# Layer 3's experts: parts of 112 and 64, and blocks finished in pairs

## The chip, the cores and the metric

The kernel runs on one core of a Trainium2 chip. The metric is the device time of one execution in microseconds (us). Before the change it is 716.23 us (median of 3 runs, 713.53 to 717.75). The experts that the change touches work in fp32.

## What is computed

A stack of four layers, each an attention or graph step and a feed-forward step, on x of 4 x 256 tokens with 256 features. The change touches only the last feed-forward step, a mixture of experts with one shared branch. On the 1024 normalized rows:

```python
H = 256; I_MOE = 176; I_SH = 704; E = 8; TOP_K = 2
probs = softmax(x @ W_router.T)
rw, sel = top_k(probs, TOP_K)
combine = zeros((T, E)).at[arange(T)[:, None], sel].add(rw)
sh = silu_and_mul(x @ Ws_gate_up, I_SH) @ Ws_down
shared_out = sh * sigmoid(x @ W_sgate.T)
gu = einsum('th,ehi->eti', x, We_gate_up)        # 2 * 176 columns
h = silu_and_mul(gu, I_MOE)                      # 176 columns
eo = einsum('eti,eih->eth', h, We_down)          # contracts over 176
out = shared_out + einsum('eth,te->th', eo, combine)
```

Each token goes to two of eight experts. An expert's hidden width is 176. Layer 2 has a step of the same kind with a hidden width of 128.

## The kernel before

**Stages.** The layers run one after the other, with some overlap at the borders. Layer 3's feed-forward step comes last: routing, a dispatch that sorts the 2048 token-expert pairs into blocks of 128 rows with one expert each, the experts over these blocks, and the shared branch, pieces of which run before and after the experts.

**Units.** `experts` (L378) does one block per unit; there are NB = 23 of them, numbered 0 to 22. A unit has four pieces:

- `load` (L382): SyncE reads the expert's number and starts the load of its weights (`d_w`, six buffers); GpSimd gathers the 128 rows by an indirect DMA (`d_x`, six buffers, L397); TensorE transposes them in two halves (L402), and one copy empties the bank into `d_xT`.
- `up`: two matmuls of 128 rows and 352 columns (the helper at L217), silu of the first 176 columns on ScalarE (L412), times the other 176 on VectorE (L413): `d_h`, 128 tokens by 176.
- `turn_round`: `d_h` must be contracted over its 176 columns, so they have to be put on partitions. There are only 128 of these, so the 176 are cut into `parts` = 2 halves of `hs` = 88. Two transposes (L420) write the halves side by side into one bank of PSUM, 88 partitions by 256 columns, and one copy empties both into `d_hT` (three buffers).
- `down`: two matmuls of 88 rows and 256 columns (L430) add up the halves in one bank, a copy takes the result to `d_y`, and GpSimd writes the rows out by an indirect DMA (L439).

The pieces are skewed: in step s TensorE gets load(s), up(s-1), turn_round(s-2), down(s-3). TensorE's order is written out by hand for this part of the kernel (`in_order`), and it waits in that order. The other engines' orders come from the tile framework's scheduler, and the waits on semaphores from its tracking of tiles.

**Copies out of PSUM.** `evac` (L104 to L111) alternates between VectorE (L109) and ScalarE (L111) with each call. In layer 3 a unit calls it three times. All eight banks of PSUM are handed out in turn by `bank()`.

**Weights.** `_blocks` on the host lays an expert's weights out as one block of 128 partitions by 1216 columns: 704 for up, and two times 256 for the two halves of down. Layer 2 uses the same functions with one part of 128 and its weights resident in SBUF.

Of the kernel before, what the change touches and what calls it, by code (L numbers as in the profile page):

```python
# [27 lines left out]
P = 128  # L28
# [5 lines left out]
E = 8  # L34
# [4 lines left out]
TOPK2 = int(S * 0.3)  # L39
SH2, RT2 = 1024, 128  # L40
SH3, RT3 = 704, 176
RH3 = RT3 // 2
ROUND = 12582912.0
NEG = -1.0e30
LOWEST = -3.0e38
# [20 lines left out]
def flamingo(ctx: ExitStack, tc: tile.TileContext, a: dict, out: bass.AP):  # L66
# [191 lines left out]
    class Dispatch:  # L258
# [118 lines left out]
        def experts(self, src, ff, parts, between, resident=None):  # L377


            hs, width = ff // parts, KC * 2 * ff + parts * D  # L380
            state = {}

            def load(n):
                first = nc.values_load(
                    self.of[0:1, n : n + 1], min_val=0, max_val=(E - 1) * P,
                    engines=[mybir.EngineType.SP if resident is None else mybir.EngineType.PE],
                    skip_runtime_bounds_check_because="the number of experts is clamped to E - 1 above",
                )
                if resident is None:
                    w = self.pool.tile([P, width], F32, tag="d_w", name="d_w", bufs=6)  # L390
                    nc.sync.dma_start(w, src[bass.ds(first, P), :])
                    cols = lambda c0, n: w[:, c0 : c0 + n]
                else:
                    first = first * (width // P)
                    cols = lambda c0, n: resident[:, bass.ds(first + c0, n)]
                xb = self.pool.tile([P, D], F32, tag="d_x", name="d_x", bufs=6)
                nc.gpsimd.indirect_dma_start(  # L397
                    out=xb, out_offset=None, in_=rows_in, in_offset=self.indices(self.token[:, n : n + 1])
                )
                pt = bank()[:, :D]  # L400
                for kc in range(KC):
                    nc.tensor.transpose(pt[:, kc * P : (kc + 1) * P], xb[:, kc * P : (kc + 1) * P], ident)  # L402
                xbT = self.pool.tile([P, KC, P], F32, tag="d_xT", name="d_xT", bufs=3)
                evac(xbT.rearrange("p k t -> p (k t)"), pt)
                state[n] = cols, xbT

            def up(n):
                cols, xbT = state[n]
                pg = bank()[:, : 2 * ff]
                project(pg, lambda kc: xbT[:, kc, :], lambda kc: cols(kc * 2 * ff, 2 * ff))  # L410
                hb = self.pool.tile([P, ff], F32, tag="d_h", name="d_h", bufs=3)
                nc.scalar.activation(hb, pg[:, :ff], AF.Silu)  # L412
                nc.vector.tensor_mul(hb, hb, pg[:, ff:])  # L413
                state[n] = cols, hb

            def turn_round(n):
                cols, hb = state[n]
                pt = bank()[:, : parts * P]
                for c in range(parts):
                    nc.tensor.transpose(pt[:hs, c * P : (c + 1) * P], hb[:, c * hs : (c + 1) * hs], ident)  # L420
                hbT = self.pool.tile([P, parts * P], F32, tag="d_hT", name="d_hT", bufs=3)
                evac(hbT[:hs], pt[:hs])
                state[n] = cols, hbT

            def down(n):
                cols, hbT = state.pop(n)
                po = bank()[:, :D]
                for c in range(parts):
                    c0 = KC * 2 * ff + c * D
                    nc.tensor.matmul(  # L430
                        po, hbT[:hs, c * P : (c + 1) * P], cols(c0, D)[:hs], start=c == 0, stop=c == parts - 1
                    )
                y = self.pool.tile([P, D], F32, tag="d_y", name="d_y", bufs=5)
                if not self.scatter:
                    nc.scalar.copy(y, po)
                    nc.scalar.dma_start(rows_out[n * P : (n + 1) * P, :], y)
                    return
                evac(y, po)
                sent = nc.gpsimd.indirect_dma_start(  # L439
                    out=rows_out, out_offset=self.indices(self.to[:, n : n + 1]), in_=y, in_offset=None  # L440
                )
                if n:
                    tc.declare_no_dep(sent.ins, group=self.name, reason="all pairs have rows of their own")
                tc.add_to_no_dep_group(self.name, sent.ins)

            for step in range(NB + 3):
                for lag, piece in enumerate((load, up, turn_round, down)):
                    if 0 <= step - lag < NB:
                        piece(step - lag)
                between(step)  # L450
# [1389 lines left out]
def _blocks(up, down):  # L1840


    n = up.shape[2]
    out = np.zeros((E, P, KC * n + down.shape[1] * D), np.float32)
    out[:, :, : KC * n] = up.reshape(E, KC, P, n).transpose(0, 2, 1, 3).reshape(E, P, KC * n)
    out[:, : down.shape[2], KC * n :] = down.transpose(0, 2, 1, 3).reshape(E, down.shape[2], -1)
    return out.reshape(E * P, -1)


def _layout(i):  # L1850
    ctx = i["ctx_512"].reshape(B * S, C)
    cw = np.zeros((C, CW_END), np.float32)
    cw[:, CW_KV0 : CW_KV0 + C] = i["L0_xattn_W_k"].T
    bk = np.zeros((P, C + 1), np.float32)
    bk[:, :C] = i["L0_xattn_b_k"]
    bk[D1::32, C] = 1.0
    wkv, wq = i["L1_xattn_Wkv_expand"], i["L1_xattn_Wq"]
    wq1 = np.zeros((D, 4 * P), np.float32)
    for h in range(H1):
        rows = slice(h * D1, (h + 1) * D1)  # L1860
        k0 = 32 * h
        cw[:, CW_K1 + k0 : CW_K1 + k0 + D1] = wkv[rows].T
        wq1[:, k0 : k0 + D1] = wq[rows].T
    cw[:, CW_V1:] = wkv[D:].T
    cw[:, CW_Q2 : CW_Q2 + C] = i["L2_xattn_Wq"].T
    cw[:, CW_K2 : CW_K2 + C] = i["L2_xattn_Wk"].T

    router = np.zeros((D, 3, 32), np.float32)
    router[:, 0, :E] = i["L0_ffn_gate_w"]
    router[:, 1, :E] = i["L2_ffn_router_w"].T  # L1870
    router[:, 2, :E] = i["L3_ffn_W_router"].T
    router[:, 2, E : E + 1] = i["L3_ffn_W_sgate"].T
    had = np.ones((1, 1), np.float32)
    while had.shape[0] < P:
        had = np.block([[had, had], [had, -had]])

    kT = np.zeros((2, 4, 32, B * S), np.float32)
    kT[:, :, :D3] = ctx.T.reshape(2, 4, D3, B * S)
    kT[:, :, D3] = 1.0
    va = np.zeros((B * S, KV3, 32), np.float32)  # L1880
    va[:, :, :D3] = ctx.reshape(B * S, KV3, D3)
    va[:, :, D3] = 1.0

    w12, w3 = i["L2_ffn_w12"], i["L2_ffn_w3"]
    gu, dn = i["L3_ffn_We_gate_up"], i["L3_ffn_We_down"]
    sgu = i["L3_ffn_Ws_gate_up"]
    ew = i["L0_ffn_expert_w"].reshape(E // 2, 2, KC, P, D).transpose(0, 3, 2, 1, 4)
    a = {
        "x": i["x"],
        "ctxT": ctx.reshape(2, 2, S, C).transpose(1, 3, 0, 2).reshape(P, 2, S),  # L1890
        "cw": np.concatenate([cw, cw]),
        "bk": bk,
        "g_xattn": i["g_xattn"],
        "g_ffn": i["g_ffn"],
        "ln_gamma": i["L0_xattn_ln_gamma"],
        "ln_beta": i["L0_xattn_ln_beta"],
        "router": router.reshape(KC, P, -1).transpose(1, 0, 2),
        "gate_b": i["L0_ffn_gate_b"],
        "expert_bias": i["L2_ffn_expert_bias"],
        "gamma_raw": i["L2_xattn_gamma_raw"].reshape(1),  # L1900
        "hadamard": had,
        "expert_w": ew.reshape(E // 2, P, KC * 2 * D),
        "expert_b": i["L0_ffn_expert_b"].reshape(E * D),
        "l1_wq": _kc(wq1),
        "l1_wo": _kc(i["L1_xattn_Wout"].T),
        "l1_w0": i["L1_ffn_w_gate"].T.reshape(KC, P, FF1),
        "l1_w1": i["L1_ffn_w_up"].T.reshape(KC, P, FF1),
        "l1_w2": i["L1_ffn_w_down"].T.reshape(2, 4, P, D).transpose(0, 2, 1, 3).reshape(2, P, FF1),
        "l3_kT": kT.reshape(2, P, B * S).transpose(1, 0, 2),
        "l3_v": va.reshape(NT, P, KV3, 32).transpose(1, 0, 2, 3),  # L1910
        "ffn2_s": _chunks((i["L2_ffn_sw1"].T, i["L2_ffn_sw2"].T), i["L2_ffn_sw3"].T, CHUNKS2S),
        "ffn2_r": _blocks(w12.transpose(0, 2, 1), w3.transpose(0, 2, 1).reshape(E, 1, RT2, D)),
        "ffn3_s": _chunks((sgu[:, :SH3], sgu[:, SH3:]), i["L3_ffn_Ws_down"], CHUNKS3S),
        "ffn3_r": _blocks(gu, dn.reshape(E, 2, RH3, D)),
    }
    return {n: np.ascontiguousarray(v) for n, v in a.items()}

# [16 lines left out]
```

## Time and profile before

| what | us |
|---|---|
| median of 3 runs | 716.23 |
| lowest, highest | 713.53, 717.75 |
| the profiled execution | 717.04 |
| its span in the profile | 715.3 |
| TensorE matmuls busy | 661.3 (92%) |
| VectorE busy | 463.8 (65%) |
| ScalarE busy | 320.2 (45%) |
| GpSimd busy | 191.8 (27%) |

The span runs from the first to the last instruction on the core; the rest of the execution's time lies around it. A matmul in fp32 is shown as two records, a transpose as one. Each record's length includes its way through the array, so records of one engine overlap; how fast they follow each other is read from their starts, or from the chain of waits, which shows each only up to where the next one takes over. PEld is the load of the stationary operand. A form such as 88*128 88x256 is a matmul with 88 rows, 128 stationary columns and 256 moving ones. L217 is a helper's line and stands for several uses, which are told apart by the tiles' names.

Layer 3's experts run from about 625 us to 683 us of the span. The groups of that stretch that the change touches:

| line, engine, tile | form | count | mean ns of one |
|---|---|---|---|
| L420 PE b<-ident,d_h | 128*88 128x128 | 46 | 273 |
| L430 PE b<-d_w,d_hT | 88*128 88x256 | 92 | 379 |
| L109 VectorE d_hT<-b | 88x256 | 12 | 421 |
| L111 ScalarE d_hT<-b | 88x256 | 11 | 367 |

### The profile page before, as it was taken

What the parts mean: (1) busy time and instruction counts of PE and PEld (TensorE: products, weight loads), DVE (VectorE), ACT (ScalarE), POOL (GpSimd) and SP (SyncE); (2) the same over time, 40 slices, a digit from 0 to 9 for tenths busy, and PEclk for the clock granted to TensorE, in tenths of its full rate; (3) what the DMA queues carried; (4) which work ended last, traced back from release to release, by engine and by line L of the source; (5) the groups of instructions that cost most, each with busy time, mean ns of one, the idle gap of its engine ahead of it and who ended that gap; (6) DMA issues with size and microseconds to landing.
All of it is one profiled execution on the core that took longest, in us unless ns stands there. A gap on an engine that the chain in (4) does not pass through costs nothing.

```text
span 715.3 us, 12096 instructions
## 1 busy us (share of the span) xinstructions
PE 661.3 (92%) x4239; PEld 395.2 (55%) x4239; DVE 463.8 (65%) x1305; ACT 320.2 (45%) x702; POOL 191.8 (27%) x270
## 2 busy tenths in 40 slices
PE   6799999889987699799999989999989998999998
PEld 3434436466655476645887457554534443677745
DVE  5798999866986688857342566787857536533334
ACT  3667764644572455631243210565655653133310
POOL 2334474122232101160651430000010001367420
PEclk9869999999997899999999998999988999999999
DMA  7400113100001300020363122200000000779833
GB/s 240 184 0 1 44 40 94 46 3 25 2 2 46 154 1 0 31 89 1 110 147 91 51 77 73 82 16 19 2 31 3 2 1 31 253 244 325 290 94 113
DMA packets 26564, 54.70 MB, mean 76 GB/s; under 512 B 5004, under 2 KB 15976, under 8 KB 26248
## 3 DMA queue, kind: packets, MB, share of 16 engines
q1 hardware_dynamic: 18680, 39.38, 16.5%
q0 software_dynamic: 4080, 11.15, 5.6%
q10 hardware_dynamic: 3744, 3.41, 1.4%
q8 instruction: 34, 0.56, 0.3%
q14 instruction: 26, 0.21, 0.1%
HBM read 43.48 MB, written 9.19 MB: 74 GB/s over the span
## 4 chain that ended last, share of the span: by engine, by line
PE 65%; DVE 15%; ACT 9%; POOL 4%; issue 3%; DMA 2%; SPq 2%; ACTq 0%; POOLq 0%; DVEq 0%
PE b L217 19%; PE b L551 7%; PE b L1638 5%; PE b L1622 5%; PE b L1583 5%; PE b L956 4%; PE b L430 4%; PE b L1102 3%; ACT xn L198 2%; ACT pT L1274 2%; DVE max L1590 2%; DVE ln_st L182 1%; DVE g_work L627 1%; SPq L1579 1%; PE b L402 1%
## 5 line engine op out<-in xcount | busy, mean ns | idle before, releaser
L217 PE MATMUL b<-xnT,w 128*128 128x512 f32 (+2 forms) x288 | 113.5, 547 | 2.1 <-ACT xnT L111 1.2
L1590 DVE TENSOR_REDUCE max<-b 128x2 f32<-128x512 f32 x128 | 80.8, 682 | 25.1 <-PE b L1622 22.7
L1629 ACT ACTIVATE pT<-b 128x512 f32<-128x512 f32 x128 | 69.1, 601 | 45.8 <-PE b L1622 45.1
L217 PEld LDWEIGHTS b<-xnT,w 128*128 128x128 f32 (+1 forms) x288 | 52.7, 187 | 53.5 <-issue 48.3
L1583 PE MATMUL b<-kT,qT 32*128 32x256 f32 x512 | 72.2, 418 | 2.0 <-DMA qT<-xnT 1.5
L1622 PE MATMUL b<-qT,kT 32*128 32x512 f32 x256 | 73.4, 671 | 0.4 <-DMA qT<-rows 0.4
L956 PE MATMUL b<-w,xnT 128*128 128x512 f32 x128 | 63.9, 656 | 0.0
L397 POOL DMA_INDIRECT d_x<-rows_in,d_token x46 | 44.2, 960 | 64.8 <-DVE d_tok L373 21.3
L1583 PEld LDWEIGHTS b<-kT,qT 32*128 32x128 f32 x512 | 43.2, 193 | 23.8 <-issue 14.6
L551 PE MATMUL b<-w,hT 128*128 128x256 f32 x224 | 55.4, 401 | 0.0
L551 PEld LDWEIGHTS b<-w,hT 128*128 128x128 f32 x224 | 42.6, 197 | 13.1 <-issue 6.7
L1638 PE MATMUL b<-pT,va 128*32 128x256 f32 x512 | 42.4, 400 | 2.5 <-ACT pT L1629 2.5
L956 PEld LDWEIGHTS b<-w,xnT 128*128 128x128 f32 x128 | 26.1, 210 | 33.0 <-issue 33.0
L198 ACT ACTIVATE xn<-x,ln_shift,ln_rstd 128x256 f32<-128x256 f32 x56 | 29.3, 592 | 33.6 <-POOL ln_shift L190 33.6
L1666 POOL TENSOR_TENSOR x<-x,att 128x256 f32<-128x256 f32 x8 | 5.6, 725 | 133.2 <-DVE att L1662 90.4
L1102 PE MATMUL b<-had,zT 128*128 128x256 f32 x128 | 32.1, 406 | 9.0 <-ACT zT L1093 7.4
L972 POOL TENSOR_TENSOR re<-re 128x512 f32<-128x512 f32 (+1 forms) x32 | 33.0, 1035 | 26.3 <-ACT re L964 25.1
L1226 DVE TENSOR_REDUCE m<-b 128x3 f32<-128x384 f32 x64 | 31.1, 549 | 13.2 <-PE b L1219 13.0
L189 POOL TENSOR_TENSOR ln_rstd<-ln_ve,neghalf 128x4 f32<-128x4 f32 (+1 forms) x15 | 14.8, 985 | 91.6 <-DVE ln_shift L187 91.3
L510 DVE TENSOR_TENSOR hT<-b,sil 128x512 f32<-128x512 f32 (+1 forms) x22 | 15.2, 689 | 34.0 <-PE b L217 27.4
L509 ACT ACTIVATE sil<-b 128x512 f32<-128x512 f32 (+1 forms) x22 | 13.1, 594 | 53.7 <-PE b L217 52.1
L1278 POOL TENSOR_SCALAR_AFFINE_SELECT pT<-pT 128x512 f32<-128x512 f32 x32 | 19.6, 637 | 59.9 <-ACT pT L1274 59.9
(320 smaller groups left out, 1264.4 us busy)
## 6 DMA issues: line engine op xcount, KB each, us to landing
d_w<-in_ffn_r_dram SPq DMA_DIRECT2D x23, 608.0 KB
w<-in_ffn_s_dram SPq DMA_DIRECT2D x13, 384.0 KB
w<-in_l_w_dram SPq DMA_DIRECT2D x6, 512.0 KB
d_wall<-in_ffn_r_dram SPq DMA_DIRECT2D x1, 3072.0 KB
rows_out<-d_y ACTq DMA_DIRECT2D x23, 128.0 KB
w<-in_expert_w_dram SPq DMA_DIRECT2D x4, 512.0 KB
rows_in<-xn SPq DMA_DIRECT2D x16, 128.0 KB
d_yt<-rows_out SPq DMA_DIRECT2D x8, 256.0 KB
```

Of the source, the lines that this page charges most:

```text
L198: nc.scalar.activation(xn, x[t0 + i], AF.Identity, bias=shift[:, i : i + 1], scale=rstd[:, i : i + 1])
L217: nc.tensor.matmul(dst, lhs(kc), rhs(kc), start=kc == 0, stop=kc == KC - 1)
L397: nc.gpsimd.indirect_dma_start(out=xb, out_offset=None, in_=rows_in, in_offset=self.indices(self.token[:, n : n + 1]))
L551: nc.tensor.matmul(po, hT[:hs, j, i * P : (i + 1) * P], w[:hs, 4 * hs : 4 * hs + D], start=j == 0, stop=j == len(ws) - 1,)
L956: nc.tensor.matmul(pe, xt[:, kc, i * P : (i + 1) * P], ws0[j][:, kc * 2 * D : (kc + 1) * 2 * D], start=False, stop=kc == KC - 1,)
L972: nc.gpsimd.tensor_add(re[:, :n, :], re[:, :n, :], re[:, n : 2 * n, :])
L1102: nc.tensor.matmul(pf[:, c // 2, (c % 2) * 2 * P : (c % 2 + 1) * 2 * P], self.zT[:, c0 : c0 + P], had2[:, n].rearrange("p s q -> p (s q)") ...
L1583: nc.tensor.matmul(pn[:, half * S : (half + 1) * S], self.qT[group(k), ah, g0 + half, qt * P : (qt + 1) * P], kT[group(k), ah, self.b * S ...
L1590: nc.vector.tensor_reduce(self.max[:, ah, qt, k, g0 : g0 + 2], pn.rearrange("p (g s) -> p g s", g=2), AX.X, ALU.max, negate=True,)
L1622: nc.tensor.matmul(pn, kT[group(k), ah, c : c + P], self.qT[group(k), ah, g0 : g0 + 2, :], start=True, stop=True)
L1629: nc.scalar.activation(self.pT[u][:, k, :], pn, AF.Exp, scale=D3**-0.5)
L1638: nc.tensor.matmul(self.acc[group(k), cols], va[:, 2 * self.b + kt, 4 * ah + k, :], self.pT[u][:, k, cols], start=kt == 0 and g == 0, stop ...
```

## The change

The 176 columns are cut into 112 and 64 instead of 88 and 88 (`first_part`). The second part of an even unit goes to partitions 0 to 63, that of an odd unit to partitions 64 to 127 (`rows`). For an odd unit the second part is written as a plain matmul with the identity as the moving operand, all other parts as transposes. Each part has a copy of its own, right after it, and `d_hT` gets four buffers.

`down` does nothing for an even unit, and in the next step does two units together: the two first parts, and then the two second parts, each in its own half of the rows of TensorE's array and in its own bank. The last unit, number 22, has no partner and is done alone. The host puts the second part's weights into both halves of the partitions. The size of a weight block, the number of loads, gathers and writes, and the order on GpSimd and SyncE stay the same. For layer 2 (one part) nothing changes.

```diff
@@ -39,7 +39,6 @@
 TOPK2 = int(S * 0.3)
 SH2, RT2 = 1024, 128
 SH3, RT3 = 704, 176
-RH3 = RT3 // 2
 ROUND = 12582912.0
 NEG = -1.0e30
 LOWEST = -3.0e38
@@ -377,7 +376,15 @@
         def experts(self, src, ff, parts, between, resident=None):
 
 
-            hs, width = ff // parts, KC * 2 * ff + parts * D
+            width = KC * 2 * ff + parts * D
+            first_part = ff - P // 2 * (parts - 1)
+
+            def rows(n, c):
+
+
+                r = P // 2 * (n % 2) if c else 0
+                return slice(r, r + (ff - first_part if c else first_part))
+
             state = {}
 
             def load(n):
@@ -416,20 +423,35 @@
             def turn_round(n):
                 cols, hb = state[n]
                 pt = bank()[:, : parts * P]
+                hbT = self.pool.tile([P, parts * P], F32, tag="d_hT", name="d_hT", bufs=4)
                 for c in range(parts):
-                    nc.tensor.transpose(pt[:hs, c * P : (c + 1) * P], hb[:, c * hs : (c + 1) * hs], ident)
-                hbT = self.pool.tile([P, parts * P], F32, tag="d_hT", name="d_hT", bufs=3)
-                evac(hbT[:hs], pt[:hs])
+                    part = rows(n, c), slice(c * P, (c + 1) * P)
+                    src = hb[:, c * first_part : ff if c else first_part]
+                    if part[0].start:
+                        nc.tensor.matmul(pt[part], src, ident, start=True, stop=True)
+                    else:
+                        nc.tensor.transpose(pt[part], src, ident)
+                    evac(hbT[part], pt[part])
                 state[n] = cols, hbT
 
             def down(n):
-                cols, hbT = state.pop(n)
-                po = bank()[:, :D]
+                if parts == 2 and n % 2 == 0 and n + 1 < NB:
+                    return
+                some = (n - 1, n) if parts == 2 and n % 2 else (n,)
+                pos = [bank()[:, :D] for _ in some]
                 for c in range(parts):
-                    c0 = KC * 2 * ff + c * D
-                    nc.tensor.matmul(
-                        po, hbT[:hs, c * P : (c + 1) * P], cols(c0, D)[:hs], start=c == 0, stop=c == parts - 1
-                    )
+                    for m, po in zip(some, pos):
+                        cols, hbT = state[m]
+                        r = rows(m, c)
+                        nc.tensor.matmul(
+                            po, hbT[r, c * P : (c + 1) * P], cols(KC * 2 * ff + c * D, D)[r],
+                            start=c == 0, stop=c == parts - 1,
+                        )
+                for m, po in zip(some, pos):
+                    del state[m]
+                    store(m, po)
+
+            def store(n, po):
                 y = self.pool.tile([P, D], F32, tag="d_y", name="d_y", bufs=5)
                 if not self.scatter:
                     nc.scalar.copy(y, po)
@@ -1840,10 +1862,15 @@
 def _blocks(up, down):
 
 
-    n = up.shape[2]
-    out = np.zeros((E, P, KC * n + down.shape[1] * D), np.float32)
+    n, ff = up.shape[2], down.shape[1]
+    parts = -(-ff // P)
+    first = ff - P // 2 * (parts - 1)
+    out = np.zeros((E, P, KC * n + parts * D), np.float32)
     out[:, :, : KC * n] = up.reshape(E, KC, P, n).transpose(0, 2, 1, 3).reshape(E, P, KC * n)
-    out[:, : down.shape[2], KC * n :] = down.transpose(0, 2, 1, 3).reshape(E, down.shape[2], -1)
+    out[:, :first, KC * n : KC * n + D] = down[:, :first]
+    if parts == 2:
+        for r in (0, P // 2):
+            out[:, r : r + P // 2, KC * n + D :] = down[:, first:]
     return out.reshape(E * P, -1)
 
 
@@ -1909,9 +1936,9 @@
         "l3_kT": kT.reshape(2, P, B * S).transpose(1, 0, 2),
         "l3_v": va.reshape(NT, P, KV3, 32).transpose(1, 0, 2, 3),
         "ffn2_s": _chunks((i["L2_ffn_sw1"].T, i["L2_ffn_sw2"].T), i["L2_ffn_sw3"].T, CHUNKS2S),
-        "ffn2_r": _blocks(w12.transpose(0, 2, 1), w3.transpose(0, 2, 1).reshape(E, 1, RT2, D)),
+        "ffn2_r": _blocks(w12.transpose(0, 2, 1), w3.transpose(0, 2, 1)),
         "ffn3_s": _chunks((sgu[:, :SH3], sgu[:, SH3:]), i["L3_ffn_Ws_down"], CHUNKS3S),
-        "ffn3_r": _blocks(gu, dn.reshape(E, 2, RH3, D)),
+        "ffn3_r": _blocks(gu, dn),
     }
     return {n: np.ascontiguousarray(v) for n, v in a.items()}
```

## The prediction

> **What bounds the kernel now.** First the chain of waits over the last 115 us, because the change sits in layer 3's experts and nowhere else. One unit of that stage in the steady part, with two pieces of the shared FFN around the stage for comparison:
>
> ```profile
> 608.14 5.96 PE b L551 x24
> ...
> 643.65 1.19 PE b L217 x4
> 644.84 0.22 PE b L420 x2
> 645.06 0.86 PE b L430 x4
> 645.92 0.22 PE b L402 x2
> ...
> 682.93 17.31 PE b L217 x40
> 700.24 11.94 PE b L551 x48
> ```
>
> Start, length, what ran, records. From 625.42 to 682.93 the chain is almost only TensorE: 23 units, each load (L402) 0.22, up (L217) 1.19, turn (L420) 0.22, down (L430) 0.865, in all 2.49 us. A 256-column fp32 matmul is two records of 0.216, a transpose one of 0.109. So a microsecond added to or taken from TensorE's order here moves the end. Next the table of stretches, for what lies just beneath:
>
> ```profile
> core 0: us, PE busy (x) PEld busy (x) DVE busy (x) ACT busy (x) POOL busy (x), PEclk, DMA share, GB/s
> 641.00:661.00 20.00, 20.00 (x99) 14.83 (x98) 7.48 (x21) 6.81 (x20) 15.13 (x16) 1.00 1.00 335
> ```
>
> TensorE is busy throughout, at clock 1.00; VectorE and ScalarE a third of the time; but the DMA engines are full too. A unit moves 608 KB of weights and two times 128 KB of rows: at 335 GB/s that is 2.64 us. There is a second bound close under the first.
>
> **What the change takes away.** Down becomes one pass for two units: two 112-row matmuls (four records, 0.864), then two 64-row matmuls, one on partitions 0 to 63 and one on 64 to 127. Do two such matmuls overlap? Layer 2's L610 does the same with eight matmuls:
>
> ```profile
> 29.44 2.00 PE L610 MATMUL b<-qkT 64*128 64x256 f32 x16 [0.15 <-DVE s_ve L811]
> ```
>
> Sixteen records of 0.216 in turn would take 3.46 us; they fit into 2.00, pipeline tail included. So I take full overlap: 0.432 for the two instead of 0.864. Gross gain: 0.432 a pair, 11 pairs, **4.75 us**.
>
> **What it adds: tile switches.** The Trainium skill, TensorEngine Tiling (Array Packing), promises up to twice the speed for contractions of 64 or fewer (Theoretical Speedup), but says that changing the tiling mode drains the engine (Key Properties), with no price. The trace has the price. L551 has one 64-row chunk in each group of six. At 608.14, 24 records at 0.216 are 5.18, the piece took 5.96: 0.78 for four switches (two groups, in and out). At 700.24, 48 records are 10.37, it took 11.94: 1.57 for eight. Both give **0.195 a switch**, of which the weight loads show the drain:
>
> ```profile
> 701.79 0.41 PEld L551 LDWEIGHTS b<-w,hT 128*128 128x128 f32 x2
> 702.53 0.29 PEld L551 LDWEIGHTS b<-w,hT 64*128 64x128 f32 x2 [0.33 <-DVE x L480]
> 703.15 0.30 PEld L551 LDWEIGHTS b<-w,hT 128*128 128x128 f32 x2 [0.33 <-issue]
> ```
>
> Into a narrower stationary (64 columns, within the piece at 682.93: 40 records of 0.429 are 17.16, it took 17.31) a switch is 0.15; before a transpose I also take 0.15. A paired down is then 0.864 + 0.195 + 0.432 + 0.15 (into the next load) = 1.64, against 1.73 for two downs before. By the rule alone the pairing gains 0.43 a pair, by the rows **0.09**: 1 us in all.
>
> **What it adds: a wait in the turn.** Before, both transposes of a unit go into one bank and one copy empties it. Now each part is copied right after its own transpose, from the same bank. The built order of the changed kernel says what follows: the second part's instruction waits for ScalarE in even units and for VectorE in odd ones, and the count it waits for is that of the copy of the first part of the same unit. TensorE runs in a fixed order, so everything queued behind it waits too: the paired down or the next load, the next up, and through them all later units. The Trainium skill, PSUM — Partial Sum Buffer, section "PSUM bank collisions raise a hardware error", says why such a wait is there: engines are kept apart by bank and group of 32 partitions, not by address, so other columns of the bank don't help. By address alone there would be no wait. Before's trace has none of this kind, so I build it from rows:
>
> ```profile
> 644.67 0.38 PE L420 MATMUL b<-ident,d_h 128*88 128x128 f32 x2
> 644.88 0.32 ACT L412 ACTIVATE d_h<-b 128x176 f32<-128x176 f32 x1 [1.03 <-PE b L217]
> 645.15 0.37 ACT L111 COPY d_hT<-b 88x256 f32<-88x256 f32 x1
> ...
> 647.58 0.42 DVE L109 COPY d_hT<-b 88x256 f32<-88x256 f32 x1 [1.20 <-PE b L420]
> ```
>
> ```profile
> 599.61 0.27 ACT L111 COPY logits<-b 128x128 f32<-128x128 f32 x1 [1.96 <-PE b L224]
> 599.93 0.14 PEld L235 LDWEIGHTS b<-ident,logits 128*128 128x128 f32 x1 [0.65 <-ACT logits L111]
> ```
>
> - Even unit. The copy on ScalarE stands behind the silu of the next unit and starts 0.48 after the first transpose, 0.37 after that one's slot. Half as wide it takes 0.26 (layer 2's 128x128 copies: mean 260 ns; fewer partitions save nothing, 88x256 took 367 and 128x256 372). TensorE restarts 0.05 after the copy's end (599.88 to 599.93), loses 0.05 more to the uncovered weight load, and does its slot of 0.109. From slot to slot 0.84 where it was 0.109: **+0.73**.
> - Odd unit. The copy is on VectorE, which is free: it starts about 0.19 after the slot (647.58, less the start at 647.17, less two slots), takes 0.29 (384.71, 128x128), restart 0.10. The part is written as a matmul with the identity and not as a transpose: two records, 0.218. In all 0.80: **+0.69**.
> - The second parts have 64 stationary columns. Switching in is inside the wait; switching out costs 0.195 before a down (even) and 0.15 before a load (odd): **+0.345** a pair.
>
> **The sum.** A pair: 0.73 + 0.69 + 0.345 - 0.09 = +1.68; eleven are 18.4. Unit 22 is alone: its wait (0.57, no silu ahead), one switch out, and a single down with two switches (+0.39): +1.15. In all **+19.6 us**. The profiled execution was 717.04 us with a span of 715.3; that gives 736.6 and a span of 734.9. The runs' median was 716.23, 0.8 below the profiled one, so I predict **736**.
>
> Costs put at nothing, and their cover. The extra copies (23 of about 0.28, on engines a third busy) cost only through the wait above. An even unit's weight buffer is freed one unit later, and two loads start together: 1216 KB at 335 GB/s with some rows between need about 5 us; the first of them is used two units later, 6.7 us at the new pace. If that fails, up waits for about a microsecond per pair, +10. GpSimd's row writes come in pairs; it takes 15.13 us in 20 now, with 0.30 between, 2.57 a unit, and has 3.3 at the new pace. Its gathers stand behind an even unit's write, which now comes one unit later; gathers run six units ahead. After the stage TensorE has 29 us of shared FFN, behind which the last rows land as now.
>
> **Rivals.**
> 1. *The pairing wins.* The wait would have to be met already when TensorE gets there, and the switches be hidden. Then -4.75 + 11 x 0.109 for the identity matmuls = -3.5; but weights cap it: 17 loads, the first released at 630.98, at 2.64 each end at 675.9, and 4.3 us of TensorE work follow (678.62 to 682.93): 680.2, 2.7 earlier than now. So 714.3, or 713.5 against the median. For it: the overlap at L610. Against: the copy can't end before the transpose it empties, and nothing stands between the two on TensorE. It decides only where the round trip stays under some 0.04 us; by the rows it is above 0.6.
> 2. *No wait, but all switches paid.* Two column switches in (0.15 each), 0.345 out, 0.109 for the second record, -0.09: +0.66 a pair, +8 in all: 724. For it: every price is measured. Against: the named wait.
> 3. *The two row tiles don't overlap*, or weights come late: +4.75 or more on my sum: 741. Against: L610.
> 4. *Waits and no switch costs*: +1.33 a pair, +15.5: 732. For it: after a wait the array is empty, and the drain out of a short tile may be partly hidden.
>
> **Chances.** My sum, with 4 as its lower edge: 0.83. Rival 3: 0.09. Rival 2: 0.05. Rival 1, or no effect by some cover that I don't see: 0.03. About 0.5% (3.6 us) is what a measurement of this kernel tells from no change. Slower by more 0.96, within it 0.02, faster 0.02. The range goes from rival 4 less a tenth of the waits to rival 3: 730 to 741.
>
> **What would show it.** Right: in the chain, ACT and DVE pieces "d_hT" between the turn's two parts, about 0.3 each and 23 in all; TensorE busy about 80% of the stage instead of all of it; a pair every 6.7 us instead of 4.98; DMA share down from 1.00 to about 0.8. Wrong: the two parts of a turn start within 0.2 of each other (rival 2); the four 64-row records of a pair start one after the other, 0.2 apart (rival 3); "DMA d_w" before L217 in the chain.

## The result and the profile after

| | before | after |
|---|---|---|
| median, us (4 runs each) | 716.99 | 732.95 |
| lowest to highest | 713.53 to 717.92 | 730.22 to 737.27 |
| profiled execution's span | 715.3 | 728.7 |
| experts, first up to the matmul after the last down | 57.35 | 73.52 |

The changed kernel takes 1.024 times as long (95% interval 1.0209 to 1.027). The experts alone are 16.2 us longer, about the difference of the medians (16.0). The two profiled spans differ by less, 13.4 us, because this execution reached the experts 3 us earlier (622.47 against 625.42). The code up to there is the same; runs of one kernel differ by as much.

The chain of waits after, for an odd unit's turn, an even unit's turn and the paired down behind it:

```profile
645.58 1.19 PE b L216 x4
646.77 0.12 PE b L433
646.89 0.02 issue
646.91 0.30 DVE d_hT L108
647.21 0.04 issue
647.26 0.43 PE b L431 x2
647.69 0.37 PE b L409 x2
648.06 1.20 PE b L216 x4
649.26 0.02 issue
649.28 0.12 ACT d_h L419
649.41 0.06 issue
649.47 0.02 ACTq L110
649.49 0.01 issue
649.50 0.27 ACT d_hT L110
649.76 0.04 issue
649.81 0.30 PE b L433
650.11 1.50 PE b L446 x8
651.61 0.37 PE b L409 x2
```

L409 is the load, L216 the up and L446 the down. Before, L420 with its two transposes was one piece of 0.22 and nothing but TensorE stood in the chain. Now the first part (646.77) is followed by the copy that empties it on VectorE, and only then by the second part (L431, the identity matmul, 647.26). In the even unit the copy is on ScalarE (649.50). From up to up (L216) a pair takes 2.48 + 3.91 = 6.39 us, against 4.98. For one pair, from 659.67 to 666.44, the chain runs through a gather that lands at 666.43, just as L431 starts. L431 reads no gathered row, and this pair takes 6.39 us as the others do, so the gather cost nothing.

The stretch of 20 us that was shown of before, now:

```profile
core 0: us, PE busy (x) PEld busy (x) DVE busy (x) ACT busy (x) POOL busy (x), PEclk, DMA share, GB/s
641.00:661.00 20.00, 17.50 (x81) 10.06 (x81) 6.35 (x20) 5.64 (x19) 12.51 (x13) 1.00 0.84 281
```

TensorE does 81 records where it did 99, at the same clock, and is busy for 17.50 of the 20 us, where the prediction had about 80%. The DMA engines fall from 1.00 to 0.84: they are fed more slowly, and they are not what holds the kernel (e8_after_10w below).

### The profile page after: what moved, and what is told of

Read it like the earlier page. It is cut to its first block, busy times and chain, and to the rows that moved or that the text cites. A ratio compares the mean times of both kernels' runs of the same rounds, so it can differ in the third digit from the quotient of the medians.

```text
span 728.7 us, 12141 instructions
## 1 busy us (share of the span) xinstructions
PE 663.9 (91%) x4250; PEld 386.4 (53%) x4250; DVE 466.0 (64%) x1316; ACT 321.4 (44%) x714; POOL 191.8 (26%) x270
## 4 chain that ended last, share of the span: by engine, by line
PE 64%; DVE 16%; ACT 9%; POOL 4%; issue 3%; DMA 2%; SPq 1%; ACTq 0%; POOLq 0%; DVEq 0%
PE b L216 19%; PE b L573 6%; PE b L1660 5%; PE b L1605 5%; PE b L1644 5%; PE b L446 4%; PE b L978 3%; PE b L1124 3%; ACT pT L1296 2%; ACT xn L197 2%; PE b L409 2%; DVE max L1612 2%; DVE ln_st L181 1%; DVE g_work L649 1%; SPq L1601 1%
## 5 line engine op out<-in xcount | busy, mean ns | idle before, releaser
L216 PE MATMUL b<-xnT,w 128*128 128x512 f32 (+2 forms) x288 | 115.3, 554 | 2.1 <-ACT xnT L110 1.2
L216 PEld LDWEIGHTS b<-xnT,w 128*128 128x128 f32 (+1 forms) x288 | 53.2, 190 | 54.8 <-issue 49.5
L978 PE MATMUL b<-w,xnT 128*128 128x512 f32 x128 | 62.3, 642 | 0.0
L1248 DVE TENSOR_REDUCE m<-b 128x3 f32<-128x384 f32 x64 | 31.2, 550 | 13.1 <-PE b L1241 12.9
L531 ACT ACTIVATE sil<-b 128x512 f32<-128x512 f32 (+1 forms) x22 | 13.1, 594 | 53.1 <-PE b L216 51.5
L1300 POOL TENSOR_SCALAR_AFFINE_SELECT pT<-pT 128x512 f32<-128x512 f32 x32 | 19.6, 637 | 61.0 <-ACT pT L1296 61.0
```

What stands on the lines that cost most here:

```text
L216: nc.tensor.matmul(dst, lhs(kc), rhs(kc), start=kc == 0, stop=kc == KC - 1)
L978: nc.tensor.matmul(pe, xt[:, kc, i * P : (i + 1) * P], ws0[j][:, kc * 2 * D : (kc + 1) * 2 * D], start=False, stop=kc == KC - 1,)
```

## The experiments

Theory A: TensorE waits, inside each turn, for the copy out of the bank it is about to write. Rival B: the 64-row matmuls of the down and their tile switches cost the time, and the wait is hidden. Rival C: weights and rows that come in twos hold TensorE up. The first four ran beside one set of runs of before (median 715.95), the next four beside another (715.83), the last beside a third (716.46). "Stage" is measured as in the table above.

**e1_late_copies.** The wait taken out of the changed kernel:

```diff
                 for c in range(parts):
                     ...
                         nc.tensor.transpose(pt[part], src, ident)
+                for c in range(parts):
+                    part = rows(n, c), slice(c * P, (c + 1) * P)
                     evac(hbT[part], pt[part])
```

> The changed kernel, but a unit's two copies stand after both of its turn's instructions, so nothing on TensorE waits between them. Theory A (the wait for the copy out of the same bank costs the time, 0.62 us in an even and 0.55 in an odd unit): a pair of units falls from 6.39 us to about 5.3 (4.98 of before, +0.40 for the odd unit's second record and two column switches, -0.08 for the paired down); the stage about 61.5 us, the run 720 to 722. Rival B (the 64-row tiles and their switches in the down cost the time, the wait is hidden): no change, pair 6.4, run 733. Rival C (weights and row writes come in twos and hold TensorE up): little change, pair above 6.

Measured: 724.30 us, ratio 1.0119 (1.0103 to 1.0136); stage 65.6. An undisturbed pair takes 2.03 + 3.27 = 5.30 us, as theory A had it to a hundredth. Two units of its chain of waits, an odd one and an even one with the down behind it:

```profile
652.11 0.11 PE b L433
652.22 0.36 PE b L431 x2
652.58 0.37 PE b L409 x2
652.95 1.19 PE b L216 x4
654.13 0.22 PE b L433 x2
654.35 1.50 PE b L448 x8
```

L448 is the down here. No copy stands between the parts of a turn. But not all pairs are undisturbed: up waits for its weights now and then (2.9 us in all by the list of waits, 1.1 in the longest), so the stage stays 4 us above what pairs of 5.30 would give. B falls. Of C there is something here; the changed kernel's list has no wait of TensorE for weights.

**e2_split_copies.** The wait put into the kernel before:

```diff
-                for c in range(parts):
-                    nc.tensor.transpose(pt[:hs, c * P : (c + 1) * P], hb[:, c * hs : (c + 1) * hs], ident)
                 hbT = self.pool.tile([P, parts * P], F32, tag="d_hT", name="d_hT", bufs=3)
-                evac(hbT[:hs], pt[:hs])
+                for c in range(parts):
+                    part = slice(0, hs), slice(c * P, (c + 1) * P)
+                    nc.tensor.transpose(pt[part], hb[:, c * hs : (c + 1) * hs], ident)
+                    evac(hbT[part], pt[part])
```

> The kernel before (88 and 88, one down per unit), but each half of a turn is copied right after its own transpose, from the same bank: the wait alone, without tiles of 64 rows and without pairs. All its first copies fall to VectorE. Theory A: +0.55 us in each of 23 units, the unit 3.04 instead of 2.49, stage about 70 us, run 729 to 730. Rivals B and C: as before, 716 to 718.

Measured: 730.42 us, ratio 1.0205 (1.0176 to 1.0235); stage 70.5, unit 3.07. No part of 64 rows and no pair is in this kernel, and it loses 14.5 us, 13.1 of them in the stage. Its chain of waits, one unit from down to down:

```profile
641.28 0.22 PE b L402 x2
641.50 1.19 PE b L217 x4
642.68 0.12 PE b L422
642.81 0.02 issue
642.83 0.30 DVE d_hT L109
643.13 0.04 issue
643.17 0.31 PE b L422
643.48 0.87 PE b L431 x4
```

L422 is the transpose here and L431 the down. A unit takes 0.58 more than before. Between the two transposes stands the copy, 0.30, with 0.06 on its two sides. Most of the rest is the first transpose itself: the copy starts after its whole length of 0.27, where in the kernel before the second transpose followed 0.11 after its start. Theory A stands: both taking the wait away and adding it alone do what it says.

**e3_window.** As e1_late_copies, and without the identity matmul. A transpose of 128 columns that ends at the last one puts columns 112 to 175 on partitions 64 to 127 by itself:

```diff
                     if part[0].start:
-                        nc.tensor.matmul(pt[part], src, ident, start=True, stop=True)
+                        nc.tensor.transpose(pt[:, part[1]], hb[:, ff - P :], ident)
```

> As e1_late_copies, and an odd unit's second part is a full transpose of the last 128 columns of d_h (48 to 175), of which partitions 64 to 127 are copied: no column tile, no second record. What is left of the change is the paired down alone. Theory A with the prices of the trace: pair 4.90 (before 4.98), last unit +0.39, stage 57 us, run 715 to 717, the same as before. If the 64-row tiles gained all of their 0.43 a pair: stage 53, held at 55 by the weights, run 713.5. Rival B: pair 6.4.

Measured: 722.29 us, ratio 1.0093 (1.007 to 1.0116); stage 63.6. A miss in the total: undisturbed pairs are 1.62 + 3.27 = 4.89, a hundredth from the sum, but from unit 7 on hardly a pair is undisturbed. The chain of waits leaves TensorE for a load:

```profile
642.85 7.55 DMA d_w<-in_ffn_r_dram
650.40 0.14 issue
650.53 1.42 PE b L216 x4
```

From its issue to its landing this load took 7.55 us, and TensorE wanted it after fewer. Before, each down freed one weight buffer; now two are freed at once, the first of them one unit late, with six buffers as before. With the wait in the turn gone, the weights are what comes late next: C, which the wait had hidden.

**e5_single_down.** e3_window with `some = (n,)` for every unit, so no pairs.

> As e3_window, but each unit's down is done alone again, with 112 and then 64 rows: every unit pays two row switches, and no two 64-row matmuls run side by side. With 0.195 a switch: down 1.25 us instead of 0.865, unit 2.88, stage about 66 us, run 725. If switches cost nothing here: stage 57.5, run 716. The difference to e3_window tells what running side by side is worth.

Measured in one run: 722.41 us; unit 2.83, stage 64.9. A down of a 112-row and a 64-row matmul, alone, costs 0.34 more than two of 88. That is the prediction's price for the two switches, 0.195 into the 64 rows and 0.15 before the next transpose; the expectation had taken 0.195 twice. Against 4.89 for an undisturbed pair, two single units take 5.66: running two 64-row matmuls side by side, with two switches saved, is worth 0.77 a pair. No wait for weights is in its chain: buffers come free one by one, and the pace of 2.83 is slower too. In the kernel before, where they also come free one by one, TensorE waited for weights at only two units (0.25 and 0.07) at a pace of 2.49.

**e6_window_10w, e7_before_10w, e4_four_10w, e8_after_10w.** Ten weight buffers (`bufs=10` for `d_w`) in e3_window, in before, in a version that does four units' downs at a time, and in the changed kernel. For the fours:

```diff
-                if parts == 2 and n % 2 == 0 and n + 1 < NB:
+                if parts == 2 and n % 4 != 3 and n + 1 < NB:
                     return
-                some = (n - 1, n) if parts == 2 and n % 2 else (n,)
+                some = tuple(range(n - n % 4, n + 1)) if parts == 2 else (n,)
```

> e3_window with ten weight buffers instead of six. In e3_window undisturbed pairs took 4.89 us, as worked out, but from unit 7 on up waits for its weights: an even unit's buffer is freed one unit later and two loads start at once. Theory A2 (the late freeing is what holds e3_window up): no such waits, pair 4.89, stage about 57.0 us instead of 63.6, run 715.5, ratio 0.999. Rival D (the DMA engines are simply full, whatever the buffers): the waits stay, only later; stage 60 or more, run 719 or more.

> The kernel before with ten weight buffers: a control for the other two. It waits for weights only at units 18 and 19 (0.25 and 0.07 us). Both theories: stage 57.0 instead of 57.35, run 715.6, within 0.1% of before.

> e6_window_10w with down done for four units at a time (four banks, d_hT six buffers): 1.73 us for the first parts, two switches, 0.86 for the second parts two by two, so 2.94 for four instead of 3.46 one by one. Five fours gain 2.6 us, the last three units nothing. If ten buffers are enough: stage 54.7, run 713.3, ratio 0.9965. If the freeing of four buffers at once starves up, or the DMA engines are full: stage 57 or more, run 716 or more.

> The changed kernel with ten weight buffers, nothing else. Its own trace shows no wait for weights, so by theory A nothing changes: pair 6.39, stage 73.5. If part of its loss were the bursts of loads, the stage would fall below 72.

| kernel | us, median | ratio to before (95%) | stage | units |
|---|---|---|---|---|
| e6_window_10w | 715.09 | 0.9976 (0.9952 to 0.9999) | 57.1 | 1.62 + 3.27 |
| e7_before_10w | 715.13 | 0.9977 (0.9952 to 1.0002) | 57.0 | 2.49 |
| e4_four_10w | 715.78 | 0.9977 (0.9946 to 1.0007) | 57.3 | 3 x 1.62 + 4.57 |
| e8_after_10w | 729.73, one run | | 73.5 | 2.48 + 3.91 |

With ten buffers every pair of e6_window_10w is 4.89, and no wait for weights is left. So the late freeing held e3_window up, and rival D falls at this pace; but not much is left above it, as the DMA engines are busy for 0.97 of the stretch from 641 to 661. e8_after_10w has the changed kernel's unit times to 0.01: weights are no part of the changed kernel's loss. And e7_before_10w, with the buffers alone, is as good as e6_window_10w with buffers and pairs. The pairs bring 0.09 us each, 0.9 up to the last unit's up, and the end of the stage loses 1.0: unit 22's down pays its own switches, and its turn waits for the silu and the product of `d_h` with nothing left for TensorE in between, because an even unit's down is put off. In e7_before_10w downs fill that time. The net is nothing. From e6_window_10w's chain, the wait at the end:

```profile
677.03 0.33 ACT d_h L419
677.36 0.02 issue
677.38 0.35 DVE d_h L420
```

The differences of the pairs split the loss of the changed kernel: 6.39 to 5.30 is the wait (1.09), 5.30 to 4.89 the identity matmul (0.41), and 4.89 against 4.98 the pairing (a gain of 0.09); together 1.41 a pair. A pair of e6_window_10w, from down to down, has only TensorE in its chain (L432 and L430 are the transposes of the turn, L447 the down):

```profile
641.36 0.37 PE b L409 x2
641.73 1.19 PE b L216 x4
642.91 0.11 PE b L432
643.02 0.11 PE b L430
643.13 0.22 PE b L409 x2
643.35 1.19 PE b L216 x4
644.53 0.22 PE b L432 x2
644.75 1.50 PE b L447 x8
```

Fours should gain more, as one pair of switches serves four units: 9.43 us, against 9.96 for four units of before, and that is what each of the first fours takes. Then, in its chain:

```profile
662.75 0.23 PE b L432 x2
662.99 0.35 issue
663.33 7.89 DMA d_x<-rows_in,d_token
671.23 0.04 issue
```

A gather of rows, issued at 663.33, lands at 671.23, and TensorE has stood for 1.15 us by then. On GpSimd it stands behind four row writes, the last two of which are:

```profile
660.78 0.97 POOL L462 DMA_INDIRECT rows_out<-d_y,d_to  x1 [0.30 <-ACT d_xT L110]
662.05 0.97 POOL L462 DMA_INDIRECT rows_out<-d_y,d_to  x1 [0.30 <-DVE d_h L420]
663.33 0.99 POOL L404 DMA_INDIRECT d_x<-rows_in,d_token  x1 [0.30 <-PE b L432]
```

Each occupies GpSimd for 0.97 and 0.30 follows: 2.56 for a gather and a write, where a unit in fours takes 2.36 on TensorE. The gain of 2.6 us is lost again: the unit of this gather takes 3.09 instead of 1.62 and the one before it 2.49, and from the last up on the stage is 0.6 longer than in e7_before_10w. Stage 57.3.

**e9_four_12x.** The fours with twelve buffers for gathered rows.

> e4_four_10w with twelve buffers for the gathered rows instead of six. In e4_four_10w fours took 9.43 us as worked out, until the gather of unit 21 came late: on GpSimd it stood behind four row writes, 1.28 us each, and landed at 671.2 just as TensorE needed it. If the late gathers alone ate the gain, more buffers let them run ahead: no wait, stage 54.7 us, run 713.4, ratio 0.995. If GpSimd is simply full (46 transfers of 1.28 us from about 615 on end at 674.6, and the row writes of the last units come after that anyway), part of the gain stays lost: stage 55.5 to 57.

Measured: 714.68 us beside 716.46 for before, ratio 0.9996 (0.9968 to 1.0025); stage 56.5. The fours still have waits in them (unit 14 took 2.61 instead of 1.62). The stage lies in the range of the second expectation, but its reason, GpSimd's rate, is not what unit 14's wait shows:

```profile
651.55 0.97 POOL L462 DMA_INDIRECT rows_out<-d_y,d_to  x1 [2.69 <-ACT d_y L110]
653.42 0.37 ACT L110 COPY d_y<-b 128x256 f32<-128x256 f32 x1 [2.15 <-DMA rows_out<-d_y,d_to]
653.69 0.38 ACT L110 COPY d_xT<-b 128x256 f32<-128x256 f32 x1
654.12 1.16 PE L216 MATMUL b<-d_w,d_xT 128*128 128x352 f32 x3 [0.82 <-ACT d_xT L110]
```

GpSimd has just been idle for 2.69 us. TensorE waits for a copy into `d_xT`, which stands on ScalarE behind a copy into `d_y`, and that one waits for a row write, issued at 645.32, to land 8.00 us later. Four downs at once take four of the five `d_y` buffers. More of these were not tried, so what fours could gain stays open. None of these versions is faster than e7_before_10w, the kernel before with ten weight buffers, by more than the runs can tell; the stage of e9_four_12x is 0.6 us shorter than that one's, and the run times don't show it.

## Why the prediction was right, and by how much it was off

Predicted 736, 730 to 741; measured 732.95. The mechanism was right: e2_split_copies shows the wait alone, e1_late_copies shows the kernel without it. By the prediction's steps, for a pair:

- **Overlap and switches in the down.** 1.64 predicted; 1.65 measured (1.50 at 650.11, and the 0.37 at 651.61 less the 0.22 of a load without a switch). The first records of the two row tiles start 6 ns apart, and the prices of 0.195 and 0.15 hold. So the gross 0.43 a pair shrinks to 0.08, where the prediction had 0.09.
- **Odd unit.** Wait, second record and switch out: +0.84 predicted, +0.86 measured.
- **Even unit.** +0.93 predicted (0.73 and 0.195), +0.64 measured. Here are both terms that were mis-sized. First, the copy starts 0.41 after the first transpose, not 0.48: in before's row it had waited for the second transpose (it starts 0.09 after that one's end, as the copies on ScalarE of e2_split_copies do), which I put down to the silu in front of it. The 0.05 that I added for an uncovered weight load doesn't show in the wait either, which is 0.62. Second, I priced a switch out of the 64-column tile at 0.195; behind the even unit's second part the next matmul starts 0.14 later (649.81 to 649.94), where a slot is 0.11, so it costs 0.03.
- **Sum.** 1.68 predicted, 1.41 measured. The 0.27 difference over eleven pairs is 3.0 of the 3.4 us by which my 19.6 exceeded the stage's 16.2.

Rival 4, waits and no switch costs, had 732 and came closer in the number. Of its free switches only the even unit's switch out was nearly free: the odd unit's and those of the down were paid.

**A cover that was wrong.** I put the weights' two-at-a-time freeing at nothing, with about 5 us from issue to landing. It did cost nothing in the changed kernel, but only because the wait makes units slow. At the pace of rival 1 a load took 7.55 us and TensorE stood. So rival 1's price was wrong as well: it let weights cap the gain at 2.7 us, and e3_window, without the wait though with the down's switches, lost 6. Rival 2 gave 724 for a kernel that pays the switches without the wait, and e1_late_copies took 724.3; but its pair is 5.30 and not 5.64, and waits for weights make up for it. The number agrees by chance.

## What to carry to other kernels

When one copy out of a bank is split in two, do all of TensorE's writes to that bank first and the copies after them (a second bank was not tried here); write, copy, write, copy cost 0.58 us a unit in e2_split_copies. Price a tile switch from the kernel's own trace before pairing small matmuls: two switches, 0.34 together, ate four fifths of the 0.43 that two side by side saved. And work that is gathered in groups frees its buffers in groups: count the time from freeing to need at the new, faster pace, not at the old one.

## What the runs showed beyond that

A transpose of 64 columns costs no switch here, though its tile is as narrow as that of the identity matmul. In e1_late_copies, where no wait hides a switch, an even unit's two transposes (654.13) take 0.22, and the down behind them 1.50, just its own records and one switch. The odd unit's identity matmul (652.22) takes 0.36, and the two transposes of the load behind it 0.37. In e6_window_10w, where a plain transpose stands in its place, these are 0.11 and 0.22. So the identity matmul costs 0.41 a pair more (2.03 against 1.62), of which its second record is only 0.11.

The transpose and the identity matmul differ in kind and in place, as the first writes to partitions 0 to 63 and the second to 64 to 127. The piece at 682.93 of before speaks for the kind: its matmuls of 64 columns write from partition 0 and still pay 0.15. No run here has a 64-column transpose at partition 64.
